# One FFN-over-SSM kernel: where each group's products into the states stand in TensorE's order

## The chip, the cores and the metric

The program runs on 1 core of one Trainium2 chip. The metric is the device time of one execution in microseconds, from the program's start on the core to its end. Before the change the median of 3 runs is 961.89 us (961.85 to 961.9).

## What is computed

The input `x` is 64 sequences of 64 channels by 1024 positions. The first half of the layer is a diagonal state-space convolution along the positions, masked by each sequence's length; the second half is a feed-forward of 64 rank-16 experts, of which each token uses the best 16; the result is added to `x`.

```python
def cond(u, length, log_dt, C, log_A_real, A_imag, D):      # B=64, H=64, L=1024
    u_m = u * (arange(L) < length[:, None])[:, None, :]
    dtA = (-exp(log_A_real) + 1j * A_imag) * exp(log_dt)[:, None]        # 64 states a channel
    K = 2 * einsum('hn,hnl->hl', Cc * (exp(dtA) - 1) / A, exp(dtA[:, :, None] * arange(L))).real
    y = irfft(rfft(u_m, 2 * L) * rfft(K, 2 * L))[..., :L] + u_m * D[:, None]
    return y * mask[:, None, :]

def ffn(x, A, B, Wr):                                        # 64 experts of rank 16, top 16
    G = zeros.at[top_idx].set(softmax(top_k(x @ Wr.T, 16)))
    h = einsum('nd,krd->nkr', x, A)
    return 2 * einsum('nkr,kdr->nd', h * G[:, :, None], B)

out = x + ffn(cond(x, ...))
```

All of it is in float32.

## The kernel before

**Groups.** The 64 channels are worked on in 8 groups (`g`) of 8 channels, and a group in 4 pairs (`i`) of channels. A sequence of 1024 positions is cut into 8 blocks of 128. For a group three things are made: `tables(g)` makes the powers of the state's decay (`w`), their transposed and scaled form (`bt`) and a Toeplitz matrix of the first 128 taps (`toep`); `conv(g)` makes the convolution `y`; `first(g)` multiplies `y` by the experts' first factor, in a one-level Strassen scheme of seven products (`seven`, line 585, tile `h`), and gates the result. After the eight groups a second stage (`second`, line 1083) does the second factor; it starts at about 617 us of the profiled execution.

**The convolution of a pair.** It goes in four steps:

1. *Into states*: `into_states(i)`, line 652. For each of two components `c` (real, imaginary) two matmuls of 64 columns each, one per channel of the pair, side by side in the array, write a product `pu` of 128 x 448. ScalarE copies it to `s[:, c]` (line 657).
2. *Recurrence*: `recur`, on VectorE (line 398): 18 small instructions a pair carry the states over the 7 chunks.
3. *Inside a block*: `inside(i)`, line 681: one matmul of the whole array per channel, `toep` by `x`, into a PSUM bank `pc`.
4. *Out of states*: `across`, line 690: matmuls of 64 rows each, two side by side in the array, add the states' part into the same banks. VectorE then multiplies `pc` by the mask into `y` (line 698).

So TensorE's matmuls stand in three forms of the array: whole (128\*128: `h`, `pc` of line 681, the transposes `pb` and `psc`), halves by columns (128\*64: `pu`, and the scores `psh` of line 760), and halves by rows (64\*128: `pc` of line 690).

**The order.** `conv` is a generator. Its caller takes steps of it, and after each `yield` runs a number of the seven products of the group before or of this group (`ahead(products, n)`), so that TensorE has products to do while VectorE does the recurrence. Within one group from 1 to 7 TensorE's order is: into states for pairs 0 and 1; three products; `pc` of pair 0 (inside, across) and into states for pair 2; one product; `pc` of pair 1 and into states for pair 3; three products; `pc` of pairs 2 and 3. The last `step(1)` of `conv(g)` is the step of `tables(g + 1)` that transposes `bt` (`pb`, line 337, copied by ScalarE at line 339). Then `gates` follows: the scores `psh` by eight pairs of matmuls, copied by ScalarE to `sh`, transposed back (`psc`), the best 16 found on VectorE, and the gates sent through DRAM (`gt_dram`) to the tiles `gx` that `finish` multiplies by. `kernels_by_vector` makes the taps (`pk`, line 309), which go by `krows` in DRAM to `toep`.

**Buffers.** Eight PSUM banks: `ps_f` (4, the products `h`), `ps_c` (2) and `ps_k` (2). Pairs take their `pu` and `pc` from `ps_c` or `ps_k`; the transposes, the scores and `pk` take `ps_k`. The states `s` have 3 buffers in `sp`; `x` has 4 buffers in `xp`, each of 512 KB, loaded by SP's queue (line 147) once the matmuls of line 681 have read the tile before; `bt` and `toep` have one buffer each. In `gates`, `sh` and `gt` share one buffer (tag `gt`), and `sc` has its own.

Engines run their instructions strictly in the order in which the tile layer's scheduler put them; tiles and semaphores hold back what isn't ready.

Of the kernel before, what the change touches and what calls it, by code (L numbers as in the profile page):

```python
# [37 lines left out]
F32 = mybir.dt.float32  # L38
# [6 lines left out]
P = 128  # L45
NB = 64
NH = 64
L = 1024
NBLK = L // P
NS = 64  # L50
NE = 64
# [3 lines left out]
HG = 8  # L55
NG = NH // HG
# [36 lines left out]
def body(ctx: ExitStack, tc, x, xo, lens, par, dvec, dgrp, at, bm, wt, cst, out):  # L93
# [141 lines left out]


    tabs = {}
    scales = {}

    def tables(g):  # L240
# [124 lines left out]
        if g:  # L365
            turn, toep = others()
            for i in (0, 2):
                turned_table(i, 2)
            yield
        V.tensor_copy(turn[:, 0:2], w[:, :, :, P])  # L370
        ts(turn[:, 2], turn[:, 1], -1.0, ALU.mult)
# [252 lines left out]
        yield  # L624


    def conv(g, steps, out):
        if g == 0:
            next(steps)
        w, bt, turn, toep = tabs.pop(g)  # L630
        if g == 0:

            s_more = yp.tile([P, NBLK * TOK], F32, tag="y", name="s_more")
        y = yp.tile([P, NBLK, NS2, HH, NB], F32, tag="y", name=f"y_{g}")
        out.append(y)
        states = {}

        def into_states(i):
            h = g * HG + 2 * i
            if h not in x_tiles:  # L640
                load_x(h)
            xt = x_tiles.pop(h)
            if g == 0 and i == GP - 1:
                s = s_more[:, : 2 * NCH * NB].rearrange("p (c k b) -> p c k b", c=2, b=NB)
            else:
                s = sp.tile([P, 2, NCH, NB], F32, tag="s", name=f"s_{g}_{i}")
            for c in range(2):

                banks, tag = (ps_c, "pc") if g and i == 1 else (ps_k, "pk")
                pu = banks.tile([P, NCH * NB], F32, tag=tag, name=f"pu_{g}_{i}_{c}")  # L650
                for hh in range(2):
                    nc.tensor.matmul(  # L652
                        pu[hh * NS : (hh + 1) * NS, :],
                        lhsT=bt[:, i, (1 - c) * P + hh * NS : (1 - c) * P + (hh + 1) * NS],
                        rhs=xt[:, hh, : NCH * NB], start=True, stop=True,
                    )
                marks["s"] = nc.scalar.copy(s[:, c], pu.rearrange("p (k b) -> p k b", b=NB))  # L657
            states[i] = xt, s

        def recur(*pairs):  # L660
            for k in range(1, NCH):
                for i in pairs:
                    s, a = states[i][1], turn[:, 0, i : i + 1]
                    stt(s[:, :, k, :], s[:, :, k - 1, :], a, ALU.mult, s[:, :, k, :], ALU.add)
                for i in pairs:
                    s, b = states[i][1], turn[:, 1, i : i + 1]
                    stt(s[:, 0, k, :], s[:, 1, k - 1, :], b, ALU.mult, s[:, 0, k, :], ALU.add)
                for i in pairs:
                    s, nb = states[i][1], turn[:, 2, i : i + 1]
                    stt(s[:, 1, k, :], s[:, 0, k - 1, :], nb, ALU.mult, s[:, 1, k, :], ALU.add)  # L670

        def inside(i):
            xt, s = states.pop(i)
            pcs = []
            for hh in range(2):
                if g == 0:
                    banks, tag = ((ps_c, "pc"), (ps_f, "pf"))[i % 2]
                else:
                    banks, tag = (ps_k, "pk") if i == GP - 2 else (ps_c, "pc")
                pc = banks.tile([P, NBLK * NB], F32, tag=tag, name=f"pc_{g}_{i}_{hh}")  # L680
                nc.tensor.matmul(pc, lhsT=toep[:, 2 * i + hh, :], rhs=xt[:, hh, :],  # L681
                                 start=True, stop=False)
                pcs.append(pc)
            return i, s, pcs

        def across(i, s, pcs, pinned=False):
            for c in range(2):
                for hh in range(2):
                    o = hh * NS
                    m = nc.tensor.matmul(  # L690
                        pcs[hh][:, NB:], lhsT=w[o : o + NS, c, i, 1:],
                        rhs=s[o : o + NS, c].rearrange("p k b -> p (k b)"),
                        start=False, stop=(c == 1),
                    )
                    if pinned:
                        tc.keep_in_program_order(m)
            for hh in range(2):
                marks["y"] = V.tensor_tensor(  # L698
                    out=y[:, :, i // 2, 2 * (i % 2) + hh, :],
                    in0=pcs[hh].rearrange("p (k b) -> p k b", b=NB), in1=mask, op=ALU.mult)  # L700

        def out_of(i):
            across(*inside(i))

        def step(n):
            for _ in range(n):
                next(steps, None)

        if g == 0:
            step(1)  # L710
        into_states(0)
        into_states(1)
        if g == 0:
            step(3)
            masks()
            first_order.close()
            step(1)
            behind_landing(toep[0:1, HG - 1, 0:1])
            fourth_sum(wa[2], wa[5])
            prep_ctx.close()  # L720
        recur(0, 1)
        if g == 0:
            into_states(2)
            into_states(3)
            first_two = inside(0), inside(1)
            across(*first_two[0], True)
            across(*first_two[1])
            recur(2, 3)
            last_two = inside(2), inside(3)
            yield  # L730
            across(*last_two[0], True)
            across(*last_two[1])
            return
        yield
        step(4)
        yield 2

        out_of(0)
        into_states(2)
        yield  # L740
        out_of(1)
        into_states(3)
        recur(2, 3)
        yield
        step(6)
        yield
        yield
        last_two = inside(2), inside(3)
        across(*last_two[0])
        across(*last_two[1])  # L750
        step(1)


    def gates(g, y):
        yf = y.rearrange("p k s h b -> p k (s h b)")

        phalf = ps_k.tile([P, TOK], F32, tag="pk", name=f"psh_{g}")
        for d in range(NBLK):
            o = (d % 2) * NE
            nc.tensor.matmul(  # L760
                phalf[o : o + NE, :], lhsT=wt_sb[:, d, :], rhs=yf[:, d, :],
                start=(d < 2), stop=(d >= NBLK - 2),
            )
        sh = gp.tile([P, TOK], F32, tag="gt", name=f"sh_{g}")

        nc.scalar.copy(sh.rearrange("e (t p) -> e t p", t=NTT), phalf.rearrange("e (p t) -> e t p", t=NTT))

        pscore = ps_k.tile([P, NTT, 2, NE], F32, tag="pk", name=f"psc_{g}")
        for t in range(NTT):
            nc.tensor.transpose(pscore[:, t].rearrange("p s e -> p (s e)"), sh[:, t * P : (t + 1) * P], ident)  # L770
        sc = gp.tile([P, NTT, NE], F32, tag="sc", name=f"sc_{g}")
        V.tensor_reduce(sc, pscore.rearrange("p t s e -> p t e s"), AX.X, ALU.add)
        m1 = gp.tile([P, NTT, 8], F32, tag="m1", name=f"m1_{g}")
        m2 = gp.tile([P, NTT, 8], F32, tag="m2", name=f"m2_{g}")
        sa = gp.tile([P, NTT, NE], F32, tag="sa", name=f"sa_{g}")
        sb = gp.tile([P, NTT, NE], F32, tag="sb", name=f"sb_{g}")
        for t in range(NTT):
            V.max(out=m1[:, t, :], in_=sc[:, t, :])
        for t in range(NTT):
            V.match_replace(out=sa[:, t, :], in_to_replace=m1[:, t, :], in_values=sc[:, t, :], imm_value=LOWEST)  # L780
        for t in range(NTT):
            V.max(out=m2[:, t, :], in_=sa[:, t, :])
        for t in range(NTT):
            V.match_replace(out=sb[:, t, :], in_to_replace=m2[:, t, :], in_values=sa[:, t, :], imm_value=LOWEST)
        tt(sb, sb, sc, ALU.not_equal)
        tt(sa, sc, m1[:, :, 0:1].to_broadcast([P, NTT, NE]), ALU.subtract)
        ex = sa
        nc.scalar.activation(ex, sa, AF.Exp)
        tt(ex, ex, sb, ALU.mult)
        den = gp.tile([P, NTT], F32, tag="den", name=f"den_{g}")  # L790
        V.tensor_reduce(den, ex, AX.X, ALU.add)
        ts(den, den, 1.0 / SCALING, ALU.mult)
        rd = gp.tile([P, NTT], F32, tag="rd", name=f"rd_{g}")
        V.reciprocal(rd, den)
        marks["ex"] = V.tensor_tensor(
            out=ex, in0=ex, in1=rd.unsqueeze(2).to_broadcast([P, NTT, NE]), op=ALU.mult)
        return ex
# [521 lines left out]
```

## Time and profile before

| | us |
|---|---|
| median of 3 runs | 961.89 |
| the profiled execution | 961.78 |
| its span, first to last instruction | 960.0 |
| outside the span | 1.8 |
| TensorE matmuls busy | 948.8 (99%) |
| VectorE busy | 729.1 (76%) |
| GpSimd busy | 332.5 (35%) |
| ScalarE busy | 152.4 (16%) |
| stage of the groups 1 to 7 and their products, until the second stage | 56 to 617 |

The granted clock of TensorE is 1.000 over the span. A busy matmul is one that is in the array's pipeline; successive matmuls overlap in the records, so what one costs is read from start to start. In rows of the profile "x16" counts records; a float32 matmul has two of them.

### The profile page before, as it was taken

What the parts mean: (1) busy time and instruction counts of PE and PEld (TensorE: products, weight loads), DVE (VectorE), ACT (ScalarE), POOL (GpSimd) and SP (SyncE); (2) the same over time, 40 slices, a digit from 0 to 9 for tenths busy, and PEclk for the clock granted to TensorE, in tenths of its full rate; (3) what the DMA queues carried; (4) which work ended last, traced back from release to release, by engine and by line L of the source; (5) the groups of instructions that cost most, each with busy time, mean ns of one, the idle gap of its engine ahead of it and who ended that gap; (6) DMA issues with size and microseconds to landing.
All of it is one profiled execution on the core that took longest, in us unless ns stands there. A gap on an engine that the chain in (4) does not pass through costs nothing.

```text
span 960.0 us, 11875 instructions
## 1 busy us (share of the span) xinstructions
PE 948.8 (99%) x4259; PEld 723.4 (75%) x4259; DVE 729.1 (76%) x1697; ACT 152.4 (16%) x302; POOL 332.5 (35%) x285
## 2 busy tenths in 40 slices
PE   7999999999999999999999999999999999999998
PEld 2476676676676676676686588888888888888887
DVE  8899899597687687687577589878956875786674
ACT  5345051311410320220101000000000000000000
POOL 0212212051051051051041022248645654854565
PEclk9999999999999999999999999999999999999999
DMA  8916244162262252244341273662683476268332
GB/s 285 231 42 183 100 129 150 45 182 87 91 190 77 88 176 94 88 134 121 102 137 57 78 259 129 247 258 78 219 307 98 165 241 208 77 220 289 116 115 104
DMA packets 68985, 143.97 MB, mean 150 GB/s; under 512 B 9472, under 2 KB 20288, under 8 KB 68928
## 3 DMA queue, kind: packets, MB, share of 16 engines
q1 hardware_dynamic: 49420, 94.40, 29.2%
q0 software_dynamic: 16864, 47.22, 15.6%
q10 hardware_dynamic: 2644, 1.61, 0.6%
q8 instruction: 33, 0.54, 0.2%
q14 instruction: 24, 0.20, 0.1%
HBM read 94.89 MB, written 47.25 MB: 148 GB/s over the span
## 4 chain that ended last, share of the span: by engine, by line
PE 97%; DVE 2%; DMA 0%; issue 0%; ACT 0%; DVEq 0%
PE h L585 41%; PE s L1083 35%; PE pc L681 6%; PE pc L690 5%; PE pu L652 5%; PE psh L760 3%; PE pb L337 1%; PE psc L770 0%; PE last L1083 0%; DMA par_sb<-in_par 0%; DVE ey L918 0%; DVE p_eq L398 0%; DVE y L698 0%; DVE f L387 0%; DVE w L387 0%
## 5 line engine op out<-in xcount | busy, mean ns | idle before, releaser
L398 DVE SCALAR_TENSOR_TENSOR s<-s,turn 128x128 f32<-128x128 f32 (+1 forms) x558 | 154.2, 325 | 21.0 <-ACT s L657 15.6
L585 PE MATMUL h<-y,waa 128*128 128x256 f32 x512 | 119.4, 382 | 0.0
L585 PE MATMUL h<-y,was 128*128 128x256 f32 x512 | 117.1, 381 | 0.0
L585 PE MATMUL h<-ty,was 128*128 128x256 f32 x512 | 116.1, 379 | 0.0
L585 PEld LDWEIGHTS h<-y,waa 128*128 128x128 f32 x512 | 95.1, 190 | 23.9 <-issue 7.6
L585 PEld LDWEIGHTS h<-y,was 128*128 128x128 f32 x512 | 96.2, 190 | 19.1 <-issue 5.7
L585 PEld LDWEIGHTS h<-ty,was 128*128 128x128 f32 x512 | 97.0, 190 | 14.6 <-issue 1.5
L845 POOL TENSOR_TENSOR hg<-h_p,gx 128x512 f32<-128x512 f32 x16 | 27.6, 1727 | 221.2 <-DVE h_p L398 217.2
L845 POOL TENSOR_TENSOR hg<-h_u,gx 128x512 f32<-128x512 f32 x32 | 47.7, 1491 | 100.7 <-DVE h_u L387 96.5
L698 DVE TENSOR_TENSOR y<-pc,mask 128x512 f32<-128x512 f32 x64 | 41.2, 683 | 45.1 <-PE pc L690 45.1
L1097 ACT COPY p<-s 128x512 f32<-128x512 f32 x28 | 16.4, 585 | 312.4 <-PE s L1083 312.4
L942 POOL TENSOR_TENSOR o<-o,acc_a 128x512 f32<-128x512 f32 x32 | 47.7, 1509 | 41.4 <-ACT acc_a L960 21.6
L818 POOL DMA_DIRECT2D gx<-gt_dram x56 | 34.1, 624 | 73.9 <-DMA gt_dram<-gt 73.8
L681 PE MATMUL pc<-x,toep 128*128 128x512 f32 x128 | 58.9, 594 | 0.0
L585 PE MATMUL h<-ty,waa 128*128 128x256 f32 x256 | 58.4, 381 | 0.0
L657 ACT COPY s<-pu 128x448 f32<-128x448 f32 x62 | 32.7, 531 | 157.0 <-PE pu L652 157.0
L585 PEld LDWEIGHTS h<-ty,waa 128*128 128x128 f32 x256 | 48.2, 190 | 9.9 <-issue 3.5
L652 PE MATMUL pu<-x,bt 128*64 128x448 f32 x256 | 53.4, 549 | 0.0
L690 PE MATMUL pc<-s,w 64*128 64x448 f32 x248 | 52.8, 555 | 0.0
L942 POOL TENSOR_TENSOR o<-o,b_room 128x512 f32<-128x512 f32 x32 | 49.1, 1556 | 9.8 <-DVE b_room L387 9.8
L387 DVE TENSOR_TENSOR o<-o,s 128x512 f32<-128x512 f32 x50 | 34.1, 681 | 23.0 <-PE s L1083 17.3
L387 DVE TENSOR_TENSOR hg<-hg 128x512 f32<-128x512 f32 x64 | 43.0, 684 | 9.2 <-POOL hg L845 8.5
(238 smaller groups left out, 1570.1 us busy)
## 6 DMA issues: line engine op xcount, KB each, us to landing
x<-in_x SPq DMA_DIRECT2D x32, 512.0 KB
hg_dram<-hg POOLq DMA_DIRECT2D x16, 1024.0 KB, 5.8
o<-in_xo SPq DMA_DIRECT2D x64, 256.0 KB
out<-o SPq DMA_DIRECT2D x63, 256.0 KB
gx<-gt_dram POOLq DMA_DIRECT2D x56, 256.0 KB, 5.4
qy<-hg_dram SPq DMA_DIRECT2D x28, 512.0 KB
r<-hg_dram SPq DMA_DIRECT2D x26, 512.0 KB
hg_dram<-hg POOLq DMA_DIRECT2D x16, 768.0 KB, 4.9
```

Source lines behind the costliest of these rows:

```text
L387: V.tensor_tensor(out=o, in0=a, in1=b, op=o_)
L398: V.scalar_tensor_tensor(out=o, in0=a, scalar=s, in1=b, op0=o1, op1=o2)
L585: nc.tensor.matmul(bank[:, ii, :], lhsT=fac[n - 1][:, k, (j + ii) * P : (j + ii + 1) * P], rhs=rf[n - 1][:, k, :], start=(first and ii == ...
L652: nc.tensor.matmul(pu[hh * NS : (hh + 1) * NS, :], lhsT=bt[:, i, (1 - c) * P + hh * NS : (1 - c) * P + (hh + 1) * NS], rhs=xt[:, hh, : NCH ...
L657: marks["s"] = nc.scalar.copy(s[:, c], pu.rearrange("p (k b) -> p k b", b=NB))
L681: nc.tensor.matmul(pc, lhsT=toep[:, 2 * i + hh, :], rhs=xt[:, hh, :], start=True, stop=False)
L690: m = nc.tensor.matmul(pcs[hh][:, NB:], lhsT=w[o : o + NS, c, i, 1:], rhs=s[o : o + NS, c].rearrange("p k b -> p (k b)"), start=False, sto ...
L698: marks["y"] = V.tensor_tensor(out=y[:, :, i // 2, 2 * (i % 2) + hh, :], in0=pcs[hh].rearrange("p (k b) -> p k b", b=NB), in1=mask, op=ALU ...
L818: i = queue.dma_start(gx[:, ii, :], gt_dram[g, c * n : (c + 1) * n, :].unsqueeze(1).to_broadcast([n, RANK, TOK]),)
L845: G.tensor_tensor(out=o, in0=a, in1=b, op=op)
L942: tc.keep_in_program_order(G.tensor_tensor(out=o, in0=a, in1=b, op=op_))
L1083: nc.tensor.matmul(bank[:, ii, :], lhsT=left_[i - 1][:, k, ii * P : (ii + 1) * P], rhs=right_[i - 1][:, k, :], start=(first and ii == rows ...
```

## The change

Four things are altered for the groups from 1 on:

- The into-states products of all four pairs stand in one stretch. `into_states` moves out of `conv` and a new function `begin(g)` calls it for the four pairs. For group 1 it is called at the start of `conv(1)`; for groups 2 to 7 at the end of `conv(g - 1)`, right after the transposes of `bt`, hence ahead of the scores of group `g - 1`.
- Pairs 0 and 1 go out of states together: `inside(0), inside(1)`, then `across` for both, and `recur(2, 3)` after.
- The fourth pair's states get a buffer of their own (`sp_more`, one buffer in a new pool, opened once the preparation's pool is closed). To make room, `sc` takes the buffer of tag `gt`.
- Pairs 0 and 2 take `ps_k` and pairs 1 and 3 take `ps_c`, both for `pu` and for `pc`.

```diff
@@ tables
                 turned_table(i, 2)
+            turned[g] = bt
             yield
@@ before conv
+    def into_states(g, i, bt, states, more):
+        h = g * HG + 2 * i
+        if h not in x_tiles:
+            load_x(h)
+        xt = x_tiles.pop(h)
+        s = more if i == GP - 1 else sp.tile([P, 2, NCH, NB], F32, tag="s", name=f"s_{g}_{i}")
+        for c in range(2):
+            banks, tag = (ps_c, "pc") if g and i % 2 else (ps_k, "pk")
...
+    def begin(g):
+        states = begun[g] = {}
+        more = fourth[0].tile([P, 2, NCH, NB], F32, tag="s_more", name=f"s_{g}_more")
+        for i in range(GP):
+            into_states(g, i, turned.pop(g) if i == GP - 1 else turned[g], states, more)
+    fourth = []
@@ conv
+        elif g not in begun:
+            begin(g)
...
-                banks, tag = (ps_c, "pc") if g and i == 1 else (ps_k, "pk")
...
-                    banks, tag = (ps_k, "pk") if i == GP - 2 else (ps_c, "pc")
+                    banks, tag = ((ps_k, "pk"), (ps_c, "pc"))[i % 2]
...
-        into_states(0)
-        into_states(1)
-        if g == 0:
+            into_states(0, 0, bt, states, more)
+            into_states(0, 1, bt, states, more)
...
             prep_ctx.close()
+            fourth.append(pool(right, "sp_more", 1, "right"))
...
-        out_of(0)
-        into_states(2)
-        yield
-        out_of(1)
-        into_states(3)
+        first_two = inside(0), inside(1)
+        across(*first_two[0])
+        across(*first_two[1])
         recur(2, 3)
+        yield
         yield
...
         step(1)
+        if g + 1 < NG:
+            begin(g + 1)
@@ gates
-        sc = gp.tile([P, NTT, NE], F32, tag="sc", name=f"sc_{g}")
+        sc = gp.tile([P, NTT, NE], F32, tag="gt", name=f"sc_{g}")
```

No matmul, copy or transfer is added or removed.

More of the change, by code (lines that the diff above doesn't have):

```diff
@@ L237, in body @@
     tabs = {}
+    turned = {}
     scales = {}
@@ L624, in seven @@
         yield
+    begun = {}
+    def into_states(g, i, bt, states, more):
[6 more added lines that the diff above has]
+            banks, tag = (ps_c, "pc") if g and i % 2 else (ps_k, "pk")
+            pu = banks.tile([P, NCH * NB], F32, tag=tag, name=f"pu_{g}_{i}_{c}")
+            for hh in range(2):
+                nc.tensor.matmul(
+                    pu[hh * NS : (hh + 1) * NS, :],
+                    lhsT=bt[:, i, (1 - c) * P + hh * NS : (1 - c) * P + (hh + 1) * NS],
+                    rhs=xt[:, hh, : NCH * NB], start=True, stop=True,
+                )
+            marks["s"] = nc.scalar.copy(s[:, c], pu.rearrange("p (k b) -> p k b", b=NB))
+        states[i] = xt, s
+    def begin(g):
[4 more added lines that the diff above has]
+    fourth = []
     def conv(g, steps, out):
@@ L631, in conv @@
         if g == 0:
-            s_more = yp.tile([P, NBLK * TOK], F32, tag="y", name="s_more")
+            more = yp.tile([P, NBLK * TOK], F32, tag="y", name="s_more")
+            more = more[:, : 2 * NCH * NB].rearrange("p (c k b) -> p c k b", c=2, b=NB)
+        elif g not in begun:
+            begin(g)
         y = yp.tile([P, NBLK, NS2, HH, NB], F32, tag="y", name=f"y_{g}")
         out.append(y)
[L636 to L647, printed above, removed]
-                banks, tag = (ps_c, "pc") if g and i == 1 else (ps_k, "pk")
[L650 to L658, printed above, removed]
+        states = begun.pop(g, {})
         def recur(*pairs):
@@ L700, in across @@
                     in0=pcs[hh].rearrange("p (k b) -> p k b", b=NB), in1=mask, op=ALU.mult)
-        def out_of(i):
-            across(*inside(i))
         def step(n):
@@ L720, in conv @@
             prep_ctx.close()
+            fourth.append(pool(right, "sp_more", 1, "right"))
         recur(0, 1)
         if g == 0:
-            into_states(2)
-            into_states(3)
+            into_states(0, 2, bt, states, more)
+            into_states(0, 3, bt, states, more)
             first_two = inside(0), inside(1)
@@ L736, in conv @@
         yield 2
-        out_of(0)
-        into_states(2)
+        first_two = inside(0), inside(1)
+        across(*first_two[0])
+        across(*first_two[1])
+        recur(2, 3)
         yield
-        out_of(1)
-        into_states(3)
-        recur(2, 3)
         yield
```

## The prediction

> **What bounds the kernel now.** I read first the page's busy times and its chain of waits, then TensorE's own order of time for one group, then ScalarE's and the loads' around the place where the change puts work. The page says:
>
> ```profile
> PE 948.8 (99%) x4259; PEld 723.4 (75%) x4259; DVE 729.1 (76%) x1697; ACT 152.4 (16%) x302; POOL 332.5 (35%) x285
> PE 97%; DVE 2%; DMA 0%; issue 0%; ACT 0%; DVEq 0%
> ```
>
> TensorE is the path for 97% of the span, and the view of waits lists none of its matmuls waiting for another engine between 56 and 546 us. So time can only be won where TensorE is busy with something that isn't streaming. The order of time of its matmuls in group 5 (columns: start, length, line, tile, form of the array, records) shows such places:
>
> ```profile
> 427.75 3.23 PE L652 MATMUL pu<-x,bt 128*64 128x448 f32 x16
> 430.90 3.72 PE L585 MATMUL h<-y,waa 128*128 128x256 f32 x16
> 434.46 3.62 PE L585 MATMUL h<-y,was 128*128 128x256 f32 x16
> 437.91 3.62 PE L585 MATMUL h<-ty,was 128*128 128x256 f32 x16
> 441.37 1.88 PE L681 MATMUL pc<-x,toep 128*128 128x512 f32 x4
> 443.18 1.77 PE L690 MATMUL pc<-s,w 64*128 64x448 f32 x8
> 444.88 1.72 PE L652 MATMUL pu<-x,bt 128*64 128x448 f32 x8
> 446.54 3.72 PE L585 MATMUL h<-ty,waa 128*128 128x256 f32 x16
> 450.09 1.88 PE L681 MATMUL pc<-x,toep 128*128 128x512 f32 x4
> ...
> 465.73 3.60 PE L681 MATMUL pc<-x,toep 128*128 128x512 f32 x8
> 469.25 3.28 PE L690 MATMUL pc<-s,w 64*128 64x448 f32 x16
> 472.46 1.09 PE L337 MATMUL pb<-cst_sb,b 128*128 128x128 f32 x8
> 473.39 0.60 PE L585 MATMUL h<-y,waa 128*128 128x256 f32 x2
> 473.99 3.65 PE L760 MATMUL psh<-y,wt_sb 128*64 128x512 f32 x16
> ```
>
> Read from start to start, the same work costs more in pieces. Sixteen records of `h` cost 3.45 us after other `h` (434.46 to 437.91) and 3.55 after `pu` (446.54 to 450.09). Eight records of `pu` cost 1.66, sixteen 3.15 and not 3.32. Eight of line 690 cost 1.70, sixteen 3.21 (469.25 to 472.46) and not 3.40. Four of line 681 cost 1.81, eight 3.52 and not 3.62. So a change of the array's form costs, for one visit: 0.16 inside a `pu` stretch (in and out), 0.20 inside a stretch of line 690, 0.10 in line 681 ahead of it, 0.10 in the `h` behind it, and 0.10 in an `h` ahead of a `pu` or `psh` (473.39 to 473.99 is 0.60 for two records, which by 3.45/16 are 0.43; the other 0.07 is taken up below).
>
> **The change part by part.**
>
> *Pairs 0 and 1 out of states together.* Removed are one visit to line 690 with line 681 ahead of it (0.20 + 0.10), two `pu` visits (2 x 0.16), and one `h` behind (0.10): 0.72 us a group. The records give 0.71 when every stretch is added up from start to start: 2 x 5.17 (441.37 to 446.54) + 2 x 0.10 before; 3.52 + 3.21 + 0.10, and 16 records of `pu` at 3.00 without their switches, after; 10.54 - 9.83. Seven groups: -4.97 us.
>
> *Into states ahead of the scores.* In the changed program's order the 32 records of `pu` are followed directly by `psh`, and both have form 128\*64. The stretch at 427.75 goes: 0.10 in the `h` ahead + 0.16 + 0.10 behind = 0.36. The 0.07 that `psh` waited for the last `y` goes too, as 6 us of `pu` now stand ahead of it. Six groups (2 to 7; group 1 has its own stretch): 6 x 0.43 = -2.58. The passage `pu` to `psh` has no row in the trace. Bounds: 0 (as between two `pu` of a stretch) and 0.16 (a visit). The form is the same, so 0; the range keeps 6 x 0.16 = 1.0.
>
> *What the first product waits for.* Before, `pu` came 20 us and more behind the transposes; now one product's two records stand between. On the clock of the boundary before (group 4 to 5):
>
> ```profile
> 398.83 1.07 ACT L339 COPY bt<-pb 128x512 f32<-128x512 f32 x2 [10.10 <-PE pb L337]
> 399.92 1.28 ACT L267 ACT_TABLE_LOAD   x1
> 402.74 0.63 ACT L267 ACTIVATE sh<-f 128x516 f32<-128x516 f32 x1 [1.53 <-DVE f L394]
> ```
>
> The two copies take 0.585 and 0.592, so the first half of `bt` is there at 399.42 and the second at 399.91. The two `h` records end the earlier form at 399.07 + 0.43 + 0.10 = 399.60. The first product needs the first half and one `ps_k` bank, so it waits 0. Its second component takes the bank of the second copy and starts at 400.40, 0.5 late enough. If the first product waited for both halves, it would cost 0.3 to 0.45 each time, 6 x 0.45 = 2.7 at most; it is kept for the range.
>
> *ScalarE in the long stretch.* Products start at 0, 0.80, 1.55, 2.31, 3.06, 3.81, 4.56 and 5.31 (0.75 apart, 0.05 more after the first); four banks in turn. A copy starts about 1.0 behind its product (428.76 against 427.75) and takes 0.53:
>
> ```profile
> 428.76 0.53 ACT L657 COPY s<-pu 128x448 f32<-128x448 f32 x1 [3.78 <-PE pu L652]
> ```
>
> Copies alone keep up (0.53 against 0.75). But in groups 3 to 6 the changed ScalarE order has the table load and the sine of the next group's tables between the third copy and the fourth. Third copy 2.5 to 3.05, load to 4.34, sine (its `f` is ready by 3.7: five VectorE rows behind `y`, and the first recurrence steps) to 4.98, fourth copy to 5.51. The eighth product needs that bank, so it starts at 5.57 instead of 5.31, and its weights aren't preloaded (0.05): 0.31, four times: +1.24. Groups 1, 2 and 7 have no such load in the middle: 0. Bounds: 0, and 4 x 1.9 = 7.6 if load and sine lay bare.
>
> A page of the Trainium skill speaks against the change here: "ScalarE: Activation LUTs", What ACT_TABLE_LOAD costs, adds a drain of some 1.38 us to each load's 1.28. By it the wait would be 1.38 longer in four groups, 5.5 us in all. The trace disagrees: in the load beside group 1's `pu`, the copy ahead ends 0.02 us before the load and the sine starts 0.01 behind it.
>
> ```profile
> 72.22 0.25 ACT L311 COPY ks<-pk 8x128 f32<-8x128 f32 x1 [1.21 <-PE pk L309]
> 72.49 1.28 ACT L267 ACT_TABLE_LOAD   x1
> 73.78 0.64 ACT L267 ACTIVATE sh<-f 128x516 f32<-128x516 f32 x1
> ```
>
> *The loads of `x`.* SP's order is unchanged: four `x`, then `krows` and `toep`. But `x` of pairs 2 and 3 is now needed at the boundary. Both are issued by 395.39, as before, and the DMA engines go quiet afterwards (columns: window, length, busy times by engine, clock, DMA share, GB/s):
>
> ```profile
> 393.31 2.08 SPq L147 DMA_DIRECT2D x<-in_x  x2
> 400.00:402.00 2.00, 2.00 (x12) 0.85 (x10) 2.00 (x6) 1.21 (x1) 0.00 (x0) 1.00 0.00 0
> ```
>
> All has landed by 400.0, and pair 2 is due at 399.60 + 3.06 = 402.66. Cost 0; without that cover every late us costs 6.
>
> *The rest, at nothing.* The scores start about 6 us later behind `pc`, and with them `psc`, the 16 best, `gx` and `pk` with `toep`. Cover: 71 products (31 us) stand between `pk` and the next `pc` in groups 3 to 7, 45 (19.4 us) in group 2; `krows` and `toep` took 2.4 us to issue (124.64 to 127.05) and stores of 768 KB 4.9 to land. `gx` is first wanted after seven further products. The recurrences gain room: both start from one stretch, 36 steps at 0.325 are 11.7 us a couple, and VectorE was busy 50.8 of 74.3 us in such a period. In group 1, its fullest (56.65 of 63), the first `pc` of line 690 moves 4.9 us back while the recurrence of pairs 0 and 1 stays. Buffers: `s` of each pair is read before the copy that refills it by the same order; `sc` in `sh`'s place waits for `psc`, which it reads anyway. GpSimd's order only moves two `gx` issues ahead of a store.
>
> *Sum.* -4.97 - 2.58 + 1.24 = -6.3. From the profiled execution's 961.78 (0.11 under the median): 955.5; against the median 955.6.
>
> **Rivals.**
>
> 1. *No wait at the eighth product* (the sine's place in the order costs nothing): -7.55, 954.3. For it: four banks; against it: the order itself.
> 2. *The boundary waits more than I count*: the first product for both halves of `bt`, or the passage to `psh` costs a visit: up to 2.7, 958.3. For it: only 0.18 us separate the copy's end (399.42) from the due time (399.60).
> 3. *Nothing won*: the sine comes as late behind its load as at 399.92 and 402.74, 2.82 us from start to start and not 1.29, in each of the four stretches: 1.53 more, 6.1 in all, so -0.2: 961.6. For it: that row; against it: there the sine waited for VectorE's `f`, and at 72.49 it followed at once. The drain on the Trainium skill's page named above would be such a delay. The same result, if joining stretches saved no switch; the 3.15, 3.21 and 3.52 us speak against that.
> 4. *Slower: the loads of pairs 2 and 3 come late.* Their place is between the last reading of line 681 and the third product, 9.35 us after issue. If the gates' eight `gx` (2 MB) fell on them at the 322 GB/s that the DMA engines moved from 392 to 394, they'd land 6.4 us later than 400.0, 3.7 late, six times 22, less the 6.3: 978. It decides from 6.3 / 6 = 1.05 us late each. For it: the load and `hg` stores share the DMA engines (share 0.98 at 394 to 396); against it: `gx` is issued 20 us later, and the store is done.
>
> **How the numbers follow.** Forecast 0.62, first rival 0.12, second 0.14, third 0.05, fourth 0.07. I predict 955.6. The range 954.0 to 958.5 holds the forecast and the first two rivals (0.88, less a tail of each). A measurement can tell 0.2%, 1.9 us, from no change. Faster: 0.62 + 0.12 + 0.14 = 0.88; the same 0.05; slower 0.07.
>
> **What would show it.** Right: per group one row of 32 records of `pu` with `psh` directly behind and no `h` between; eight and sixteen records in lines 681 and 690 twice; these stretches at 3.52 and 3.21; a wait of about 0.3 us inside the `pu` row in groups 3 to 6, put down to the copies of line 657. Wrong: waits of `pu` for DMA `x` or for `bt`; waits of line 690 for `s`; a `psh` of 3.58 behind `pu` instead of about 3.43 + 0.10; a second stage that starts less than 6 us earlier than 617.

## The result, and the profile after

The changed kernel takes 955.42 us (median of 6 runs, 955.13 to 956.0) against 961.84 for the kernel before (median of 6 beside them): a ratio of 0.9934, 95% interval 0.9921 to 0.9947. Predicted were 955.6, with a range of 954.0 to 958.5. The profiled execution took 955.27 us with a span of 953.5; before it was 961.78 and 960.0, so the span gives the 6.5 us.

The page's busy times and its chain of waits:

```profile
PE 942.5 (99%) x4259; PEld 725.4 (76%) x4259; DVE 714.3 (75%) x1697; ACT 150.8 (16%) x302; POOL 332.5 (35%) x285
PE 42%; DVE 0%; issue 0%; DVEq 0%
```

TensorE issues the same 4259 records in 6.3 us less of busy time: what went was no work and almost no idle time, but time inside "busy". The chain looks different (97% before) only because this one is followed back no further than the last group's `psh` at 542 us; for what lies ahead of it, the order of time has to be read. Here it is for TensorE, at the boundary on whose clock the prediction was worked out, in the period behind it and at the next boundary (columns: start, length, line, tile, form of the array, records). Counted by the scores `psh`, which come once a group from group 0 on, the first is the boundary of groups 5 and 6; the prediction calls it 4 to 5, and its row at 427.75 belongs to group 6 and not 5. No sum of it depends on that.

```profile
394.58 0.59 PE L587 MATMUL h<-y,waa 128*128 128x256 f32 x2
395.11 6.45 PE L642 MATMUL pu<-x,bt 128*64 128x448 f32 x32
401.38 3.60 PE L772 MATMUL psh<-y,wt_sb 128*64 128x512 f32 x16
404.92 1.13 PE L587 MATMUL h<-y,waa 128*128 128x256 f32 x4
...
439.67 3.60 PE L695 MATMUL pc<-x,toep 128*128 128x512 f32 x8
443.20 3.28 PE L704 MATMUL pc<-s,w 64*128 64x448 f32 x16
446.40 3.72 PE L587 MATMUL h<-ty,waa 128*128 128x256 f32 x16
449.96 3.62 PE L587 MATMUL h<-y,was 128*128 128x256 f32 x16
...
467.99 0.60 PE L587 MATMUL h<-y,waa 128*128 128x256 f32 x2
468.51 6.23 PE L642 MATMUL pu<-x,bt 128*64 128x448 f32 x32
474.58 3.60 PE L772 MATMUL psh<-y,wt_sb 128*64 128x512 f32 x16
```

What to see, from start to start:

- `psh` stands directly behind 32 records of `pu`. It takes 3.53 us (401.38 to 404.92), where before, behind `h`, it took 3.58.
- The two records of `h` ahead of `pu` take 0.53, where those ahead of `psh` took 0.60.
- Pairs 0 and 1 are one stretch, 3.53 of line 695 and 3.21 of line 704.
- The long `pu` stretch takes 6.28 us at 395.11 but 6.06 at 468.51. The first is one of the four (groups 3 to 6) with a wait in the middle; the second has none.

ScalarE's order of time in the stretch at 395.11 points to the wait's cause:

```profile
397.63 0.53 ACT L647 COPY s<-pu 128x448 f32<-128x448 f32 x1 [0.22 <-PE pu L642]
398.18 1.28 ACT L268 ACT_TABLE_LOAD   x1
399.47 0.63 ACT L268 ACTIVATE sh<-f 128x516 f32<-128x516 f32 x1
400.01 1.38 ACT L647 COPY s<-pu 128x448 f32<-128x448 f32 x3
```

The table load and the sine stand ahead of the fourth copy. It starts 2.38 us behind the third, where 0.75 is the products' pace, and the eighth product needs the bank that it empties. The last stretch of `h`, which no wait interrupts until the second stage, starts at 546.68 instead of 553.21: all of the gain, 6.53 us, is made by then.

### The profile page after: what moved, and what is told of

The parts are those of the page before. It is cut to its first block, busy times and chain, and to the rows that moved or that the text cites. A ratio compares the mean times of both kernels' runs of the same rounds, so it can differ in the third digit from the quotient of the medians.

```text
span 953.5 us, 11891 instructions
## 1 busy us (share of the span) xinstructions
PE 942.5 (99%) x4259; PEld 725.4 (76%) x4259; DVE 714.3 (75%) x1697; ACT 150.8 (16%) x302; POOL 332.5 (35%) x285
## 5 line engine op out<-in xcount | busy, mean ns | idle before, releaser
L400 DVE SCALAR_TENSOR_TENSOR s<-s,turn 128x64 f32<-128x64 f32 (+1 forms) x432 | 118.9, 320 | 3.5 <-ACT s L647 2.4
L389 DVE TENSOR_TENSOR h_u<-h,h_u 128x512 f32<-128x512 f32 x48 | 32.8, 683 | 35.3 <-PE h L587 35.3
L642 PE MATMUL pu<-x,bt 128*64 128x448 f32 x256 | 51.1, 545 | 0.0
L954 POOL TENSOR_TENSOR o<-o,u 128x512 f32<-128x512 f32 x36 | 45.3, 1281 | 10.0 <-DVE u L389 9.7
```

Of the source, the lines that this page charges most:

```text
L389: V.tensor_tensor(out=o, in0=a, in1=b, op=o_)
L400: V.scalar_tensor_tensor(out=o, in0=a, scalar=s, in1=b, op0=o1, op1=o2)
L642: nc.tensor.matmul(pu[hh * NS : (hh + 1) * NS, :], lhsT=bt[:, i, (1 - c) * P + hh * NS : (1 - c) * P + (hh + 1) * NS], rhs=xt[:, hh, : NCH ...
L954: tc.keep_in_program_order(G.tensor_tensor(out=o, in0=a, in1=b, op=op_))
```

## The experiments

All are edits of the changed kernel. The theory says that a change of the array's form has a price, that the joined stretches save it, and that ScalarE's table load gives part of it back. The main rival is that the form has no price and the gain comes from elsewhere.

**Scores apart.** The call that puts the next group's products into states ahead of the scores is taken out; they stand by themselves again at the next group's start.

```diff
         step(1)
-        if g + 1 < NG:
-            begin(g + 1)
```

> The changed kernel with one part undone: the products into states stand in a stretch of their own again at the start of each group (one h product between them and the scores); pairs 0 and 1 out of states stay together. No table load or sine lies between the copies of a stretch in this order. Theory (each change of the array's form is paid, 0.43 us for the visit that joining saved, six groups; the wait inside the stretch, 0.21 us in four groups, goes): 955.4 + 2.6 - 0.85 = 957.2 us. Rival (the form changes have no price and the gain came from elsewhere): 954.6 to 955.4 us. The record of psh should be 3.58 us again with an h ahead of it, and the pu row about 6.06 us in every group.

Measured: 957.12 us. TensorE's order of time:

```profile
396.06 0.59 PE L587 MATMUL h<-y,waa 128*128 128x256 f32 x2
396.66 3.65 PE L770 MATMUL psh<-y,wt_sb 128*64 128x512 f32 x16
400.24 2.42 PE L587 MATMUL h<-y,waa 128*128 128x256 f32 x10
...
424.73 6.23 PE L642 MATMUL pu<-x,bt 128*64 128x448 f32 x32
430.89 3.72 PE L587 MATMUL h<-y,waa 128*128 128x256 f32 x16
```

`psh` is at 3.58 and the two `h` ahead of it at 0.60 again. The `pu` stretch takes 6.16 in every group, 0.10 over the expected 6.06, since it now ends in a change of form. The `h` behind it pays another 0.10. The 1.70 us more are 6 visits less the 0.85 of waiting that this order hasn't: 0.425 a visit, where 0.43 was predicted. Of that some 0.07 is `psh`'s wait for the last `y`, which is back too, and the rest, 0.35, the form. The rival falls.

**Pairs apart.** Pairs 0 and 1 go out of states one after the other, with one product of `h` between; the rest stays.

```diff
-        first_two = inside(0), inside(1)
-        across(*first_two[0])
-        across(*first_two[1])
-        recur(2, 3)
+        across(*inside(0))
         yield
+        across(*inside(1))
+        recur(2, 3)
         yield
```

> The changed kernel with the other part undone: pairs 0 and 1 go through the group's matmuls one after the other (line 695's inside, the states, the products of h between), the scores stay behind the products into states. Theory: a visit to the 64*128 form more with its way in and out, 0.20 + 0.10 + 0.10 = 0.40 us in each of seven groups, 955.4 + 2.8 = 958.2 us. Rival (no price for a form change): 955.4 us.

Measured: 958.01 us, 2.59 more, 0.37 in each of seven groups against 0.40 expected.

```profile
441.59 1.88 PE L695 MATMUL pc<-x,toep 128*128 128x512 f32 x4
443.40 1.77 PE L704 MATMUL pc<-s,w 64*128 64x448 f32 x8
445.11 3.72 PE L587 MATMUL h<-ty,waa 128*128 128x256 f32 x16
448.67 1.88 PE L695 MATMUL pc<-x,toep 128*128 128x512 f32 x4
450.48 1.77 PE L704 MATMUL pc<-s,w 64*128 64x448 f32 x8
452.18 3.72 PE L587 MATMUL h<-y,was 128*128 128x256 f32 x16
```

Two pieces of 1.81 and two of 1.70 stand for 3.53 and 3.21, and two stretches of `h` instead of one pay 0.10: 0.39 by the records. The other part of that term, the two `pu` visits of a group that went into the long stretch, was not undone by itself; it stands on the traces alone.

**A change of form by itself, and its control.** Ahead of each of the four products of pairs 2 and 3 in groups 1 to 7 stands one small matmul more, of the whole array or, in the control, as two halves in the form that the products have. These results are read by nobody.

```diff
+            if g and i > 1:
+                nc.tensor.matmul(pu[:, NCH * NB :], lhsT=ident, rhs=xt[:, 0, :NB], start=True, stop=True)
```

> The changed kernel with 28 matmuls more: in groups 1 to 7, ahead of each of the four products into states of pairs 2 and 3, one matmul of the whole array (form 128*128, 64 columns) into columns of the same bank that nobody reads; its result is used nowhere, and the rest is complete. It measures the disputed cost by itself: each of them leads out of the 128*64 form and back. Theory (a way out and back costs about 0.30 us, and the 64 columns some 0.055, worked out as a fifth of the 0.27 us that 320 columns less cost elsewhere: an estimate): 28 x 0.36 = 9.9 us, of which up to 0.85 lies under the wait for the copy behind the sine: 964.5 to 965.3 us. Rival (no price for the change of form): 28 x 0.055 = 1.5, 956 to 957 us.

```diff
+            if g and i > 1:
+                for hh in range(2):
+                    nc.tensor.matmul(pu[hh * NS : (hh + 1) * NS, NCH * NB :],
+                                     lhsT=ident[:, hh * NS : (hh + 1) * NS],
+                                     rhs=xt[:, 0, :NB], start=True, stop=True)
```

> The control to the run before it: the same 28 places, but each with two matmuls of the half-array form 128*64 that the products around them have, 64 columns each, into the same unread columns. No change of form. Both theories: 28 x about 0.06 us = 1.7 us, less up to 0.85 under the wait for the copy: 956.3 to 957.1 us. If it came near the run before it, the extra time there would be that of additional matmuls and their weights and not of the form.

Measured: 969.19 us with the whole array, 957.66 with halves. TensorE's order of time, first of the one, then of the control:

```profile
408.48 0.43 PE L642 MATMUL pu<-x,cst_sb 128*128 128x64 f32 x2
408.84 0.97 PE L645 MATMUL pu<-x,bt 128*64 128x448 f32 x4
409.74 0.44 PE L642 MATMUL pu<-x,cst_sb 128*128 128x64 f32 x2
```

```profile
399.87 0.28 PE L643 MATMUL pu<-x,cst_sb 128*64 128x64 f32 x4
399.98 0.92 PE L648 MATMUL pu<-x,bt 128*64 128x448 f32 x4
400.73 0.28 PE L643 MATMUL pu<-x,cst_sb 128*64 128x64 f32 x4
```

One round takes 1.27 us with the whole array (408.48 to 409.74) and 0.87 with halves (399.87 to 400.73). The array works through the same number of columns in both, and the whole-array matmuls cost 0.41 us more each ((969.19 - 957.66) / 28). The rival, 956 to 957 us, falls.

Not all of the 0.41 need be the form's, for the weights differ too. In the first trace the two loads of the whole-array weights (128 columns) start 0.11 us apart (408.47 and 408.58), whereas loads of the halves (64 columns) follow one another after 0.05 to 0.06 in both traces. With no change of form the whole-array matmul could therefore take up to 2 x 0.11 = 0.22, an estimate from these rows, where the control's takes 0.12 (0.87 less the 0.75 of a product). A way out of the form and back is then worth between 0.31 and 0.41. These two runs don't narrow it further; the 0.35 to 0.39 of the two runs before lie between.

Both runs came out above their expectations, 13.8 us more than the changed kernel instead of 9.9, and 2.2 instead of at most 1.7. What is sure to have been too small is the work of the 64 columns, 0.055, as each of these matmuls leaves two records. By the rows, 28 x 0.53 (0.12 and 0.41) less the 0.85 of waiting that disappears under them is 14.0.

**The sine behind the copies.** The next group's table load and the two sines go behind all eight copies of line 647 in ScalarE's order.

```diff
-        nc.scalar.activation(sh, f, AF.Sin, scale=math.pi)
-        nc.scalar.activation(sn, f, AF.Sin, scale=2.0 * math.pi)
+        with tc.issue_after(marks["s"].ins) if g > 1 else ExitStack():
+            nc.scalar.activation(sh, f, AF.Sin, scale=math.pi)
+            nc.scalar.activation(sn, f, AF.Sin, scale=2.0 * math.pi)
```

> The changed kernel with the next group's table load and sine moved behind all eight copies out of pu in ScalarE's order (groups 2 and later); TensorE's order is unchanged. Theory (the eighth product waits for the copy that stands behind load and sine): the gap of 0.21 us in groups 3 to 6 goes, 955.4 - 0.85 = 954.6 us, and the pu row is 6.06 us in every group from 2 on. Rival (the gap has another cause, such as the bank's release or VectorE): 955.4 us with the gap still there. A second risk: the tables come later and a row behind them waits, which would show as a wait of VectorE and, if it reaches TensorE, as more than 955.4.

Measured: 954.85 us; its profiled execution lost 1.0 us elsewhere, where line 696 waited for `toep`, so it was run again beside the changed kernel.

> The changed kernel itself once more, on one chip with the two runs that follow, so that their differences don't hang on the chip: 955.4 us by both theories.

> The kernel of the third run again (the table load and the sine behind all eight copies). Theory (0.21 us of waiting in each of four groups goes): 0.85 us under the changed kernel on the same chip, 954.6 us. Rival (what the wait gave back is lost again in the second stage, as the third run's profiled execution was no shorter in its span): within 0.2 us of the changed kernel.

Measured on one chip: 955.27 us for the changed kernel, 954.62 with the sine behind. Of the second, TensorE's order of time at the same boundary:

```profile
394.60 6.23 PE L643 MATMUL pu<-x,bt 128*64 128x448 f32 x32
400.67 3.60 PE L773 MATMUL psh<-y,wt_sb 128*64 128x512 f32 x16
404.20 1.56 PE L588 MATMUL h<-y,waa 128*128 128x256 f32 x6
405.60 0.66 PE L783 MATMUL psc<-cst_sb,sh 128*128 128x128 f32 x4
```

The stretch takes 6.06 us: the wait is gone, so its cause was the load and the sine between the copies. Of the expected 0.85 only 0.65 came. The rest shows in `psc`: six records of `h` stand ahead of it instead of four and its own length is 0.66 instead of 0.60, as the copy of `sh` now stands behind the sines and the squares on ScalarE. By the records each of the four `psc` costs 0.055 more: 4 x (0.212 - 0.055) = 0.63.

**The transposes earlier.** With the sine behind the copies, `pb` is also put between line 697 and line 706 of pairs 2 and 3 (in banks of another pool), where the array has its form already.

```diff
-            pb = ps_k.tile([P, n, 2 * P], F32, tag="pk", name=f"pb_{g}_{i}")
+            banks, tag = (ps_f, "pf") if g > 1 else (ps_k, "pk")
+            pb = banks.tile([P, n, 2 * P], F32, tag=tag, name=f"pb_{g}_{i}")
...
         last_two = inside(2), inside(3)
+        step(1)
         across(*last_two[0])
         across(*last_two[1])
-        step(1)
```

> The sine behind the copies as in the run before, and also the transposes pb set ahead of line 704's products of pairs 2 and 3 instead of behind them (in banks of another pool), so that the order is 128*128 (line 695, pb), 64*128 (line 704), 128*64 (pu, psh): one visit to the 128*128 form less in six groups. Theory: pb between line 704 and pu costs 0.10 + 0.06 on the way in and 0.14 with the two h's on the way out, of which 0.15 is left when line 704 leads straight to pu: 6 x 0.15 = 0.9, so 955.4 - 0.85 - 0.9 = 953.7 us. Rival (only the number of long stretches counts, not each change of form): 954.6 us. If the other pool's banks are not free in time, pb waits and the time is above 954.6.

Measured: 956.79 us, not 953.7: a miss, by a wait that the expectation hadn't seen. VectorE's order of time, with the `pu` stretch beginning at 396.33:

```profile
394.76 0.87 DVE L402 SCALAR_TENSOR_TENSOR f<-cst_sb,p_tulo,f 128x129 f32<-128x129 f32 x3
395.55 1.28 DVE L714 TENSOR_TENSOR y<-pc,mask 128x512 f32<-128x512 f32 x2
396.74 0.34 DVE L402 SCALAR_TENSOR_TENSOR f<-cst_sb,p_tulo,f 128x129 f32<-128x129 f32 x1
397.12 0.43 DVE L398 TENSOR_SCALAR f<-f 128x516 f32<-128x516 f32 x1
397.47 1.28 DVE L714 TENSOR_TENSOR y<-pc,mask 128x512 f32<-128x512 f32 x2
```

Products into states take over the banks that the four `y` of line 714 empty. With the transposes gone from between, `pu` follows line 706 at once, and rows of the next tables stand ahead of these `y`: the first product comes 0.15 us late (0.57 in group 2), the third 0.37, in five groups. The cure is to hold those rows behind the `y`:

```diff
         yield
-        step(4)
+        with tc.issue_after(marks["y"].ins):
+            step(4)
         yield 2
```

> The fourth run with its waits taken away: the transposes pb ahead of line 704's products of pairs 2 and 3, the sine behind the copies, and the rows of the next tables on VectorE held behind the four y of pairs 2 and 3 in VectorE's order. In the fourth run two such rows stood between the y of pair 2 and of pair 3, and the third product into states (0.37 us) and the first (0.15 us) waited for the banks that these y read, 0.52 us in five groups, 2.6 us. Theory: those waits go, 956.8 - 2.6 = 954.2 us, with a pu row of 6.06 us behind a row of line 704 of 3.21 in every group from 2 on. Rival (the banks come free late anyway, as the transposes were what covered the y): 956 us or more, with the third product's gap still there.

> The kernel of the eighth run again. Theory (0.85 us of waits and 6 x 0.15 = 0.9 us of changes of form less): 1.75 us under the changed kernel on the same chip, 953.7 us, with an interval against before that doesn't reach that of the changed kernel. Rival (the eighth run's chip was the faster one): within 0.5 us of the changed kernel.

Measured: 953.45 us (ratio 0.9907, 0.9892 to 0.9922), and again 953.45 on the chip on which the changed kernel took 955.27: 1.82 less, where 1.75 were expected. (It is 0.7 under the 954.2, as the run with the waits had lost 0.4 more in group 2 and 0.055 in each of five `psc`, which the expectation left in.) The ratios there are 0.9909 (0.9896 to 0.9922) and 0.9941 (0.9919 to 0.9962), so the two intervals do touch, against the expectation; of the single runs the slowest of the one, 953.65, is below the fastest of the other, 955.14. TensorE's order of time in the second run:

```profile
385.45 3.60 PE L697 MATMUL pc<-x,toep 128*128 128x512 f32 x8
388.89 1.04 PE L340 MATMUL pb<-cst_sb,b 128*128 128x128 f32 x8
389.85 1.77 PE L706 MATMUL pc<-s,w 64*128 64x448 f32 x8
391.46 1.67 PE L706 MATMUL pc<-s_more,w 64*128 64x448 f32 x8
393.06 6.23 PE L644 MATMUL pu<-x,bt 128*64 128x448 f32 x32
```

From line 697 to `pu` it is 7.61 us; in the changed kernel 8.19, of which 0.43 are the two `h` that now stand elsewhere: 0.15 a group, six times, as worked out. This version beats both kernels.

**The loads of `x` made late.** The `x` of pairs 2 and 3 is loaded twice into its tile, the second time behind the first.

```diff
+            if i > 1:
+                load_x(g * HG + 2 * i)
+                again = x_tiles[g * HG + 2 * i]
+                nc.sync.dma_start(again, x[g * HG + 2 * i : g * HG + 2 * i + 2].rearrange("h p c -> p h c"))
             into_states(g, i, turned.pop(g) if i == GP - 1 else turned[g], states, more)
```

> The changed kernel with the x of pairs 2 and 3 loaded twice into the same tile, the second load behind the first, so that its last bytes land some us later: the fourth rival's mechanism, made on purpose. The outputs are complete. Theory (the loads have a cover that ends at about 3 us in the boundary's stretch, and whatever is late beyond it is paid six times): pair 3's second load lands some 14 us after the last reading of its room, due at 12.75, so 1 to 2 us late six times: 961 to 969 us, with a wait of the pu row for DMA. If the loads have more cover than I counted: 955.4 us and no such wait.

Measured: 959.36 us (958.41 to 962.18), between the two expectations. TensorE's order of time at the start of group 2:

```profile
119.02 3.23 PE L642 MATMUL pu<-x,bt 128*64 128x448 f32 x16
125.03 3.23 PE L642 MATMUL pu<-x,bt 128*64 128x448 f32 x16 [2.79 <-DMA x<-in_x]
```

This is the only wait of `pu` for `x` in the profiled execution: pair 2's first product starts 2.96 us late there, where stores of `hg` run beside the loads (388 GB/s in all in the window 121 to 123 us). In groups 3 to 7 even the doubled load landed in time. So the mechanism is real: the last stretch of `h` starts 3.06 us later than in the changed kernel, the wait and little else. Another 0.6 us of the span came up behind it, in the second stage, and is not explained.

How wide the cover is depends on the group. In the changed kernel's own trace the last packet of `x` ends 3.2 to 4.1 us before pair 2's first product is due in groups 3 to 7, but only 1.75 in group 2 (120.26, due at 122.01). That is the group in which twice the load used it up.

## Why the prediction was right, point by point

- *Pairs 0 and 1 together, -4.97.* Right where it was undone: 0.37 to 0.39 for the piece that was worked out as 0.40. Its `pu` part (2 x 0.16) was only read, not undone.
- *Into states ahead of the scores, 6 x 0.43.* Right: 0.425 by undoing it. The passage from `pu` to `psh` was taken at 0 between bounds of 0 and 0.16; the next record follows after 0.369 us, as between two records within the `pu` stretch, so it is 0. `psh`'s wait for the last `y` went as well. Together the records of both terms give -7.46 us against -7.55.
- *The wait at the eighth product, 4 x 0.31.* The mechanism, the four groups and the copy were right. The size was not: 0.212 each, 0.85 us in all, a third less than the predicted 1.24. From the start of the stretch the third copy came at 2.52 (predicted 2.5), the load at 3.07 (3.05), the sine at 4.36 (4.34), but the fourth copy at 4.90 (4.98). A ScalarE row of 0.63 hands over to the next after 0.54, as 399.47 to 400.01 shows, and the prediction had added its length. That is most of the difference of 0.10.
- *The first product's wait, taken at 0:* right. The first load of its weights is put down to the copy of `bt` in the changed kernel, and to nothing in the kernel before, where `bt` had been there for 20 us; the idle time ahead of it is 0.33 in both (first the kernel before, then the changed one):

```profile
427.74 0.20 PEld L652 LDWEIGHTS pu<-x,bt 128*64 128x64 f32 x4 [0.33 <-issue]
395.11 0.20 PEld L642 LDWEIGHTS pu<-x,bt 128*64 128x64 f32 x4 [0.33 <-ACT bt L340]
```

From the last start of `h` to the first record of `pu` it is 0.31 in both, too. So `bt` came in time and cost nothing.

- *The rest, at nothing:* right for TensorE's matmuls. Between 56 and 546 us the view of waits lists one of them, the last group's `psh` for `y`, 0.31, which the kernel before had as well, and the stretch of `h` behind that runs to the second stage without one.
- *The sum.* -7.46 + 0.85, and 0.08 by which all stood later before the first change, is -6.53 against -6.3. The wait was 0.39 smaller than predicted; 0.09 less saved by the forms and the 0.08 go the other way. That the median came within 0.2 of the 955.6 is in part luck, as these errors partly cancel; without it, the forecast would still lie well inside its range.
- *The rivals.* The first (no wait) was 1.1 us off, and moving the sine makes it nearly true. The second falls with the passage and the first product's wait at 0. The third falls with the sine 1.29 us behind the start of its load. (By the drain that the Trainium skill's page "ScalarE: Activation LUTs", What ACT_TABLE_LOAD costs, adds to each load, the wait would by estimate have been 1.38 us longer than predicted; the trace disagrees, with 0.212 in all.) The fourth was not met; its mechanism was seen only with the loads doubled, and in one group.

## What to carry to other kernels

Where TensorE is "busy" for 99%, read its rows from start to start: the same sixteen records cost more behind another form of the array, and putting rows of one form side by side wins that back without touching any work. Then look at what the joined rows hang on: banks that another engine must empty, and anything long that stands between its copies. A filler between two stages may be the cover for a slower engine; before it is moved, ask which bank it gave time to.

## What the runs showed of the hardware

- A change of the array's form and back costs 0.35 to 0.39 us around the long stretches of this kernel (undone 6 and 7 times), and between 0.31 and 0.41 around a matmul of 64 columns (28 times, against a control in the form of its surroundings).
- Rows of one form need not be of one kind: `psh` (512 columns, other weights, another line) follows `pu` (448) after 0.369 us, like another record of `pu`.
- The records of the weight loads show a difference between the two cases. `psh`'s first load behind `pu` starts 0.37 us ahead of its first matmul (401.01 and 401.38), whereas `pu`'s first load behind `h` starts with it (395.11 for both). That part of the price of the form lies there is likely, but no run separates it. The first load of `psh`:

```profile
401.01 0.14 PEld L772 LDWEIGHTS psh<-y,wt_sb 128*64 128x64 f32 x2 [0.24 <-ACT s L647]
```

- A ScalarE row of 0.63 us lets the next start after 0.54; lengths added up overstate a chain of such rows.
